# One attention and feed-forward layer in float32: constant rows filled by engines instead of DMAs, both first pairs stacked ahead, and three reorderings of the steady step

## The chip, the cores and the metric

The kernel runs on one core of a Trainium2 chip. The core has a matrix engine (TensorE, PE in the profile, with its weight loads as PEld), a vector engine (VectorE, DVE), an engine for activation functions (ScalarE, ACT), a general one (GpSimd, POOL), and a queue processor (SyncE, SP) that here only issues DMAs. Each engine works through its own instructions in the order in which the program gives them. They meet through semaphores.

The metric is the device time of one execution in microseconds. Three runs of the kernel before give a median of 858.41 us (858.38 to 859.41).

## The reference

The input is 32 sequences of 256 tokens with 128 features. What is computed, cut to what matters:

```python
def attn(x):                       # 16 heads of 8 features
    Q, K, V = heads(x @ Wq.T + bq), heads(x @ Wk.T + bk), heads(x @ Wv.T + bv)
    scores = Q @ K.T / sqrt(8)
    delta = t[:, None] - t[None, :]
    scores = where(delta < 0, -inf, scores) + where(delta < 0, 0, -delta)
    return heads_back(softmax(scores) @ V) @ Wo.T + bo

def ffn(x):                        # the weights are -8, 0 or 8, one scale for each output
    h = silu((x @ w1.T) * s1) * ((x @ w2.T) * s2)      # 128 -> 512
    h = gelu((h @ h1.T) * sh1)                         # 512 -> 512, exact gelu
    h = gelu((h @ h2.T) * sh2)                         # 512 -> 512
    return (h @ w3.T) * s3                             # 512 -> 128

x = layernorm(x + attn(x))
x = layernorm(x + ffn(x))
```

## The kernel before, in words

**Pairs and steps.** Two sequences make a pair: 512 tokens, four tiles of 128 (NT = 4). There are 16 pairs. `step(n)` (line 691) does the softmax of pair n, the row maxima of pair n+1, the projections of pair n+2, the last layer and last norm of pair n-2, and then the feed-forward layers of pair n-1. Every engine executes in program order, and that order is written out by hand: work is put into generators, and a `next()` puts its next piece of instructions where the call stands. `InOrder` (line 48) keeps the order of four engines as written, so that all their instructions carry line 56 in the profile.

**Scores.** Heads are worked in 8 groups of two. `qs[n % 2]` and `ks[n % 2]` (lines 109 and 110) are tiles of 128 partitions x 8 groups x 512 tokens, in which each half of the partitions holds one head's stacked rows: a high and a low part of q or k, which `project` and `halves` (315, 296) make and `stack` (306) moves in with 4 DMAs of 256 KB each per tensor; constant rows, which carry the distance term and a separation of the two sequences; and, in rows 62 and 63, the negated row maxima. With these rows one matmul yields finished scores. Before, the constant rows come about thus: DVE and POOL zero the four tiles (lines 111, 116, 670, 671), POOL makes small tiles of 4 x 512 (`constants`, 169), and 20 DMAs of 32 KB copy them into all groups (`stack_rows`, 204; `ones` for rows 62 and 63 of k).

**Row maxima.** `row_maxima(n, i)` (372), for i = 0 to 11, puts the scores of a third of two groups into a PSUM tile (`s`, from a pool of three) and has DVE reduce it into `m`. `maxima_to_rows(n)` (405) transposes `m` on PE (`pm`), splits it into a high and a low part on ACT and DVE (`mhi`, `mlo`) and moves them into q's rows 62 and 63 with four DMAs of 16 KB. Only then can pair n's softmax start.

**Softmax and outputs.** `weigh(n, i)` (424) makes the scores again, ACT takes the exponential (`e`), and POOL cuts the triangle. `outputs(n, a)` (462) is the product with the values (`pa`); for odd a, ACT copies it (`oT`), PE transposes it (`pt`) and DVE divides (`rec`, `on`). `finish(n)` (507) transposes (`pon`), copies (`onT`), multiplies by the output weights (`po`) and adds the input.

**Layer norms.** `layernorm` (265) has two pieces: statistics on DVE and a power on POOL, then the scaling on DVE. `first_norm` gives `x1`, `turn` transposes it, and `last(n)` (643) is the last layer (`pw` from `heven`), its scale (`yT`), a transposition back (`py`), the addition (`y`), the last norm (`z`, in four pieces in all) and the store.

**Feed-forward.** `feed(n)` (554) has twelve points at which other work is let in (`yield`): four in the first, gated layer, and four in each of the two inner layers. The weights are exact in the reduced float32r format; an activation is split into a high and a low part, so each product is two matmuls. An inner layer takes its outputs o in three passes, (0, 1), (2) and (3); the first pass does inner blocks k = 0, 1, 2 of output 0, then of output 1, and then k = 3 of both. The work let in is `rest()` (722) of `step`: the last outputs with their division, `maxima_to_rows(n + 1)`, `finish`, `project_values(n + 2)`, `first_norm`.

**Step 0** has no feed-forward work. It converts the weights to float32r and counts what differs (`inexact_weights`, 617; ACT casts and DVE `differ`, eleven pieces); the count (`pcount` on PE) decides the branch.

**The start** (lines 667 to 689): for pairs 0 and 1 in turn, project, zero, stack, add the constant rows, project the values; then the twelve row maxima of pair 0, `maxima_to_rows(0)`, the loads of the layers, and LEAD = 3 row maxima of pair 1.

Of the kernel before, what the change touches and what calls it, by code (L numbers as in the profile page):

```python
# [17 lines left out]
P = 128  # L18
# [11 lines left out]
W = 8  # L30
# [4 lines left out]
LEAD = 3  # L35
# [24 lines left out]
def tile_attn_ffn(  # L60
# [50 lines left out]
    vec.memset(qs[0].bitcast(F32), 0.0)  # L111
    ident = const.tile([P, P], F32, name="ident")
    make_identity(nc, ident)
    half = const.tile([P, NT], F32, name="half")
    nc.gpsimd.memset(half, -0.5)
    nc.gpsimd.memset(ks[0].bitcast(F32), 0.0)
# [14 lines left out]
    sctx = ctx.enter_context(ExitStack())  # L131
    setup = sctx.enter_context(tc.tile_pool(name="setup", bufs=1))
# [19 lines left out]
    act.dma_start(out=wv_sb, in_=wvT)  # L152
    act.dma_start(out=bv_sb, in_=bv.to_broadcast([P, D]))
    act.dma_start(out=bo_sb, in_=bo.to_broadcast([P, D]))
    for a in range(G):
        act.dma_start(
            out=wo_sb[C * HD * a : C * HD * (a + 1), :],
            in_=woT[:, :, a, :].rearrange("c d o -> (c d) o"),
        )
    for raw, dst in zip(raws, (wq_sb, wk_sb)):  # L160
        vec.tensor_copy(
            dst.rearrange("i (p d g) -> i p d g", p=2, g=W),
            raw.rearrange("i (g p d) -> i p d g", p=2, g=W),
        )
    vec.tensor_scalar(wq_sb, wq_sb, HD**-0.5, None, ALU.mult)
    vec.tensor_scalar(bq_sb, bq_sb, HD**-0.5, None, ALU.mult)


    def constants(step, one, value, lo, hi, nm):

        t = setup.tile([4, TOK], F32, name=nm)
        nc.gpsimd.iota(
            t, pattern=[[0, 2], [step, T]], base=0, channel_multiplier=0,
            allow_small_or_imprecise_dtypes=True,
        )
        nc.gpsimd.affine_select(
            out=t, in_=t, pattern=[[0, TOK]], base=1, channel_multiplier=-1,
            compare_op=ALU.is_ge, fill=0.0,
        )
        nc.gpsimd.affine_select(  # L180
            out=t, in_=t, pattern=[[0, TOK]], base=-one, channel_multiplier=1,
            compare_op=ALU.not_equal, fill=1.0,
        )
        u = setup.tile([4, TOK], F32, name=nm + "_mask")
        nc.gpsimd.memset(u, value)
        nc.gpsimd.affine_select(
            out=u, in_=u, pattern=[[0, 2], [1, T]], base=2 * P - lo, channel_multiplier=-P,
            compare_op=ALU.is_ge, fill=0.0,
        )
        nc.gpsimd.affine_select(  # L190
            out=u, in_=u, pattern=[[0, 2], [-1, T]], base=hi - 2 * P, channel_multiplier=P,
            compare_op=ALU.is_ge, fill=0.0,
        )
        nc.gpsimd.tensor_tensor(t, t, u, ALU.add)
        return t

    ones = setup.tile([2, TOK], F32, name="ones")
    nc.gpsimd.memset(ones, 1.0)
    const_rows = {
        "q": constants(-1, 0, 1.0, 0, 63, "qconst"),  # L200
        "k": constants(1, 1, BIG, 64, 127, "kconst"),
    }

    def stack_rows(dst, r, rows, eng):

        for p in range(2):
            eng.dma_start(
                out=dst.bitcast(F32)[64 * p + r : 64 * p + r + 2, :, :],
                in_=rows.unsqueeze(1).to_broadcast([2, W, TOK]),
            )  # L210

    def stack_constants(dst, nm, eng):
        for e in range(2):
            stack_rows(dst, W * e, const_rows[nm][2 * e : 2 * e + 2, :], eng)
# [157 lines left out]
    def row_maxima(n, i):  # L372
# [29 lines left out]
        for p in range(2):  # L402
            mask(s[:, p].rearrange("i h b j -> i (h b) j"), p, 0, 4)
        vec.tensor_reduce(
            mv[:, :, 2 * a : 2 * a + 2, :, 0], s, AX.X, ALU.max, negate=True
        )

    def maxima_to_rows(n):

        q, m = pairs[n]["q"], pairs[n]["m"]  # L410
        pm = work(f"pm_{n}")
# [419 lines left out]
```

## Time and profile before

| what | value |
|---|---|
| median of three runs | 858.41 us |
| the profiled execution's own time | 859.17 us |
| its span | 857.4 us, 17396 instructions |
| mean granted TensorE clock | 0.956 |
| busy: PE, DVE, ACT, POOL | 799.5, 635.0, 519.5, 270.9 us |
| first matmul of row maxima, pair 0 | 31.81 us |
| first matmul of the softmax, pairs 0, 1, 2 | 55.14, 91.23, 142.27 us |
| one steady step | 48.9 us |
| granted clock from 36.9 to 85.8 and from 85.8 to 134.6 us | 0.67, 0.83 |

The profiled execution's own time is 1.8 us longer than its span; the difference lies around the span. A step is the same to a few hundredths of a microsecond from pair 2 to pair 13, so one of them stands for all: the text uses the one from 377 to 426 us. The start up to about 135 us and the last two pairs are read apart.

### The profile page before, as it was taken

The numbers are of one execution on the slowest core, as the hardware profiler recorded it, in microseconds if no ns is written. First come the engines' busy times: TensorE is split into PE (matmuls) and PEld (weight loads), VectorE is DVE, ScalarE is ACT, GpSimd is POOL, SyncE is SP. The second block draws the span as 40 slices with busy tenths as digits, with TensorE's granted clock in tenths as the row PEclk, the third lists the DMA queues.
The fourth block names the chain that finished last, engine by engine and source line by source line (L and its number), as shares of the span: only waits on it lengthen the run. The fifth ranks groups of instructions, "written<-read, shape, count | busy, mean of one in ns | idle before, by whom it ended". The sixth has DMA issues, their size and how long they took to land.

```text
span 857.4 us, 17396 instructions
## 1 busy us (share of the span) xinstructions
PE 799.5 (93%) x7042; PEld 561.5 (65%) x7042; DVE 635.0 (74%) x1231; ACT 519.5 (61%) x713; POOL 270.9 (32%) x354
## 2 busy tenths in 40 slices
PE   4588999999999999999999999999999999999895
PEld 2355667676766767676766767676676767666673
DVE  3677677878778686878778787878778687874664
ACT  1026367666576676657676666657666666658462
POOL 9123332414232241414233240524224141424200
PEclk9558699999999999999999999999999999999998
DMA  6543240220405041140404032040504013000001
GB/s 142 128 147 86 45 101 16 61 67 14 102 14 114 14 101 26 38 90 14 103 13 112 16 74 54 14 102 14 115 13 111 5 48 68 14 5 13 1 1 29
DMA packets 40627, 48.16 MB, mean 56 GB/s; under 512 B 4376, under 2 KB 22040, under 8 KB 40536
## 3 DMA queue, kind: packets, MB, share of 16 engines
q1 hardware_dynamic: 38240, 44.13, 21.8%
q10 hardware_dynamic: 2296, 2.82, 1.4%
q8 instruction: 57, 0.93, 0.5%
q14 instruction: 34, 0.28, 0.1%
HBM read 7.48 MB, written 4.19 MB: 14 GB/s over the span
## 4 chain that ended last, share of the span: by engine, by line
PE 63%; DVE 24%; ACT 5%; issue 3%; DMA 2%; POOL 2%; ACTq 0%; DVEq 0%; POOLq 0%
PE peven L56 13%; PE s L56 9%; PE podd L56 9%; DVE m L56 9%; PE pw L56 8%; PE pa L56 8%; DVE h L56 5%; DVE h0w L56 3%; PE s_0d L56 2%; DVE z L56 2%; PE s_3d L56 2%; PE po L56 2%; PE pq L56 2%; PE pv L56 2%; ACT sg L56 1%
## 5 line engine op out<-in xcount | busy, mean ns | idle before, releaser
L459 POOL TENSOR_SCALAR_AFFINE_SELECT e<-e 128x512 f32<-128x512 f32 x128 | 82.5, 644 | 275.2 <-ACT e L56 275.2
L56 DVE TENSOR_REDUCE m<-s 128x4 f32<-128x1024 f32 x128 | 155.5, 1218 | 16.3 <-PE s L56 16.1
L56 ACT ACTIVATE e<-s 128x1024 f32<-128x1024 f32 x128 | 130.9, 1022 | 55.8 <-PE s L56 26.9
L56 PE MATMUL podd<-h,h_near 128*128 128x512 f32 x512 | 142.8, 414 | 3.8 <-DVE h L56 3.4
L56 PE MATMUL peven<-hodd,h_near 128*128 128x512 f32 x512 | 122.1, 395 | 0.0
L56 PEld LDWEIGHTS podd<-h,h_near 128*128 128x128 f32 x512 | 91.7, 190 | 37.1 <-DVE h L56 20.8
L56 PEld LDWEIGHTS peven<-hodd,h_near 128*128 128x128 f32 x512 | 95.9, 188 | 23.4
L56 ACT ACTIVATE hodd<-podd,sh 128x512 fp32r<-128x512 f32 x64 | 44.1, 689 | 76.3 <-PE podd L56 76.3
L56 DVE TENSOR_TENSOR heven<-evenw,heven 128x512 fp32r<-128x512 f32 x64 | 44.3, 693 | 48.0 <-ACT evenw L56 47.5
L56 PE MATMUL pw<-x1T,w_near 128*128 128x512 f32 x256 | 75.5, 418 | 0.9 <-DVE h0w L56 0.9
L56 PEld LDWEIGHTS s<-qs,ks 64*128 64x128 f32 x512 | 39.9, 191 | 55.3 <-issue 28.4
L56 PE MATMUL s<-qs,ks 64*128 64x256 f32 x512 | 67.0, 339 | 6.5 <-DVE m L56 6.4
L56 PE MATMUL pa<-e,vaug 128*32 128x256 f32 x1024 | 71.5, 393 | 0.1
L56 DVE SCALAR_TENSOR_TENSOR h0w<-pw,s,sg 128x512 f32<-128x512 f32 x64 | 47.9, 748 | 30.1 <-ACT sg L56 30.1
L275 POOL TENSOR_TENSOR rsa<-rsa,half 128x4 f32<-128x4 f32 x16 | 16.5, 1033 | 169.6 <-DVE rsa L56 169.5
L56 ACT ACT_TABLE_LOAD x47 | 60.3, 1283 | 3.4 <-issue 2.6
L56 PE MATMUL s<-ks,qs 62*128 62x256 f32 x512 | 59.1, 309 | 2.7 <-DVE m L56 1.4
L56 ACT ACTIVATE sg<-pw,s 128x512 f32<-128x512 f32 x64 | 43.8, 685 | 28.1 <-PE pw L56 27.7
L56 ACT ACTIVATE heven<-peven,sh 128x512 fp32r<-128x512 f32 x48 | 33.4, 696 | 39.0 <-PE peven L56 39.0
L576 POOL TENSOR_TENSOR h<-h0w,h 128x512 fp32r<-128x512 f32 x31 | 40.0, 1290 | 52.6 <-DVE h L56 52.6
L56 PEld LDWEIGHTS pw<-x1T,w_near 128*128 128x128 f32 x256 | 43.4, 188 | 18.1 <-ACT nothing L56 5.8
L56 DVE TENSOR_TENSOR hodd<-oddw,hodd 128x512 fp32r<-128x512 f32 x64 | 44.0, 688 | 13.9 <-ACT oddw L56 13.7
(145 smaller groups left out, 1425.8 us busy)
## 6 DMA issues: line engine op xcount, KB each, us to landing
qs<-qhi SPq DMA_DIRECT2D x32, 256.0 KB
qs<-qlo SPq DMA_DIRECT2D x32, 256.0 KB
ks<-khi SPq DMA_DIRECT2D x28, 256.0 KB
ks<-klo SPq DMA_DIRECT2D x28, 256.0 KB
x<-in_x_dram SPq DMA_DIRECT2D x16, 256.0 KB
out_dram<-z SPq DMA_DIRECT2D x16, 256.0 KB
ks<-khi ACTq DMA_DIRECT2D x4, 256.0 KB
ks<-klo ACTq DMA_DIRECT2D x4, 256.0 KB
```

The lines of the kernel that those rows point to most:

```text
L56: return lambda *args, **kw: self.tc.keep_in_program_order(call(*args, **kw))
L275: nc.gpsimd.tensor_tensor(rs, rs, half, ALU.pow)
L459: nc.gpsimd.affine_select(out=on_diagonal, in_=on_diagonal, pattern=[[0, on_diagonal.shape[1]], [1, P]], base=0, channel_multiplier=-1, co ...
L576: (nc.gpsimd if o < (1 if final else 2) else vec).tensor_tensor(h[:, 1, o, :], whole, h[:, 0, o, :].bitcast(F32), ALU.subtract)
```

## The change

It has these parts.

1. **Constant rows.** No tile is zeroed and no constant row is moved by DMA. POOL makes a column `row` (0 to 63, twice) and a tile `number` (the token number, 128 x 512). DVE works out eleven small columns from `row` and, with three instructions of 128 x 512 each for q and k, a tile whose per-partition rows are the constants. `fill` writes this tile into all 8 groups in one instruction of 128 x 4096: ks[0] by ACT, qs[0] and qs[1] by DVE, ks[1] by POOL.
2. **Both pairs first.** Projections and stacks of pairs 0 and 1 come first, then `project_values(0)`; the four loads of the output weights go behind the stacks on ACT's queue. The rearranged copies of Wq and Wk and the scaling of bq move from DVE to ACT.
3. **Maxima in halves.** `m` is laid out so that groups 0 to 3 and 4 to 7 can be moved apart. Pair 0's first half is moved after six row maxima, with `project_values(1)` and the layer loads beside it. LEAD is 2, and pair 1's maxima are moved within step 0's loop. Pair 2's row maxima run three places later in step 1 (LAG), with the last three among the inner layers. Step 0's weight conversion begins one place earlier. Pair 2's k stack goes by ACT's queue.
4. **Inner passes row by row.** For every inner block k and each part, the matmuls of the outputs follow one another.
5. **Division behind the last gate.** One more `yield` puts the division of the last outputs behind the fourth gated output; `project_values` goes ahead of `finish`.
6. **Last norm among inner layers.** From step 2 on, the last norm of pair n-2 (statistics, power, scaling, store) goes from the softmax loop to the end of `rest()`.

The diff, cut to its core:

```diff
+LEAD, LAG = 2, 3
...
-    vec.memset(qs[0].bitcast(F32), 0.0)
+    row = setup.tile([P, 1], F32, name="row")
+    for p in range(2):
+        nc.gpsimd.iota(
+            row[64 * p : 64 * p + 64, :], pattern=[[0, 1]], base=0, channel_multiplier=1,
...
+    number = setup.tile([P, TOK], F32, name="number_of")
+    nc.gpsimd.iota(
+        number, pattern=[[0, 2], [1, T]], base=0, channel_multiplier=0,
...
+    for raw, dst, scale in zip(raws, (wq_sb, wk_sb), (HD**-0.5, 1.0)):
+        act.activation(
+            dst.rearrange("i (p d g) -> i p d g", p=2, g=W),
+            raw.rearrange("i (g p d) -> i p d g", p=2, g=W), AF.Copy, scale=scale,
+        )
...
+    def constants(nm, col):
+        t = setup.tile([P, TOK], F32, name=f"{nm}const")
+        vec.tensor_scalar(t, number, col["lo"], col["value"], ALU.is_ge, ALU.mult)
+        vec.scalar_tensor_tensor(t, number, col["hi"], t, ALU.is_le, ALU.mult)
+        vec.scalar_tensor_tensor(t, number, col["slope"], t, ALU.mult, ALU.add)
+        fills[nm] = t, col["base"]
+
+    def fill(dst, nm, eng, groups=slice(0, W)):
+        t, base = fills[nm]
+        to = dst[:, groups, :]
+        t = t.unsqueeze(1).to_broadcast([P, groups.stop - groups.start, TOK])
+        if eng is act:
+            act.activation(to, t, AF.Identity, bias=base)
+        else:
+            eng.tensor_scalar(to, t, base, None, ALU.add)
...
+    constants("k", k)
+    fill(ks[0], "k", act)
...
-                for ks in ((0, 1, 2), (3,)):
-                    for o in os:
-                        for k in ks:
-                            product(
-                                ph[o], w[:, k, o * P : (o + 1) * P],
-                                [h[:, i, k, :] for i in parts], k == 0, k == KC - 1,
+                for k in range(KC):
+                    for i in parts:
+                        for o in os:
+                            pe.matmul(
+                                ph[o], lhsT=w[:, k, o * P : (o + 1) * P], rhs=h[:, i, k, :],
+                                start=k == i == 0, stop=k == KC - 1 and i == parts[-1],
                             )
...
+    ahead = project(0)
+    next(ahead)
+    constants("q", q)
+    fill(qs[0], "q", vec)
+    run(ahead)
+    stack(0, "q", sp)
+    stack(0, "k", act)
+    fill(ks[1], "k", nc.gpsimd)
+    ahead = project(1)
+    next(ahead)
+    fill(qs[1], "q", vec)
+    run(ahead)
+    stack(1, "q", sp)
+    stack(1, "k", act)
+    project_values(0)
...
-    for i in range(3 * G):
+    for i in range(6):
         row_maxima(0, i)
-    maxima_to_rows(0)
+    project_values(1)
+    maxima_to_rows(0, (0,))
     loaded = load_layers(once)
+    for i in range(6, 3 * G):
+        row_maxima(0, i)
+    maxima_to_rows(0, (1,))
     load_scales()
...
-            j = i if n else i + LEAD
-            if n + 1 < NPAIR and j < 3 * G:
+            j = i + {0: LEAD, 1: -LAG}.get(n, 0)
+            if n + 1 < NPAIR and 0 <= j < 3 * G:
                 row_maxima(n + 1, j)
...
-            if i in (0, 2, 4, 6) if n else i:
+            if i in ((0, 2) if n > 1 else (0, 2, 4, 6)) if n else i < 11:
                 next(settling, None)
...
+            if n == 0 and i == 3 * G - LEAD:
+                maxima_to_rows(1)
+        if n < 2:
+            run(settling)
...
-            stack(n + 2, "k")
+            stack(n + 2, "k", sp if n else act)
...
         def rest():
-            yield from side
+            for _ in range(3):
+                next(side)
+                yield
+            if n == 1:
+                for i in range(3 * G - LAG, 3 * G):
+                    row_maxima(2, i)
+                    yield
+            if 0 < n < NPAIR - 1:
+                maxima_to_rows(n + 1)
+            run(side)
             yield
-            if n + 1 < NPAIR:
-                maxima_to_rows(n + 1)
+            if n + 2 < NPAIR:
+                project_values(n + 2)
                 yield
             last_steps = finish(n)
             next(last_steps)
             yield
-            if n + 2 < NPAIR:
-                project_values(n + 2)
-                yield
             yield from last_steps
...
+            if n > 1:
+                yield
+                yield from settling
```

## The prediction

> **What bounds the kernel now.** I read the page first (shares, granted clock), then the chain of waits, then each engine's timeline of the start, of one steady step (377 to 426 us) and of the end, and the busy time in windows of the clock.
>
> The page:
>
> ```profile
> PE 799.5 (93%) x7042; PEld 561.5 (65%) x7042; DVE 635.0 (74%) x1231; ACT 519.5 (61%) x713; POOL 270.9 (32%) x354
> ...
> PEclk9558699999999999999999999999999999999998
> ```
>
> PE is nearly always busy, and a weight load stands beside every matmul. The second line shows the granted clock in 40 slices of 21.4 us: half in slices 2 and 3, low in slice 5. So the kernel has a slow start and then a long PE-bound part. A steady step, by windows (PE, PEld, DVE, ACT, POOL busy):
>
> ```profile
> 378.90:427.80 48.90, 48.06 (x442) 33.94 (x441) 38.46 (x77) 32.22 (x44) 15.63 (x20) 1.00 0.25 56
> ```
>
> Only 0.84 us of 48.9 is shown as PE idle, so relieving DVE can bring no more than PE's own stalls. They are read in PE's timeline, with the waits in brackets:
>
> ```profile
> 405.24 0.50 PE L56 MATMUL s<-qs,ks 64*128 64x256 f32 x4 [0.51 <-DVE m L56]
> ...
> 417.07 3.79 PE L56 MATMUL podd<-h,h_near 128*128 128x512 f32 x13
> 421.10 0.97 PE L56 MATMUL podd<-h,h_near 128*128 128x512 f32 x3 [0.23 <-DVE h L56]
> ```
>
> The first is the softmax loop waiting for DVE. The second hides more than its 0.23: 32 `peven` matmuls take 7.46 us in the chain, 0.233 each, so 16 `podd` from 417.07 should end at 420.8, but the chain shows `pon` only at 422.06. Some 1.0 us (after its short pipeline tail) is lost there, for k = 3. Why it is late stands in DVE's timeline:
>
> ```profile
> 417.71 0.69 DVE L56 TENSOR_TENSOR h<-h0w,h 128x512 fp32r<-128x512 f32 x1
> 418.32 0.35 DVE L56 RECIPROCAL rec<-pt 128x32 f32<-128x32 f32 x1
> 418.71 0.49 DVE L56 TENSOR_TENSOR on<-pt,rec 128x128 f32<-128x128 f32 x2
> 419.11 0.74 DVE L56 SCALAR_TENSOR_TENSOR h0w<-pw,s,sg 128x512 f32<-128x512 f32 x1
> ```
>
> The division stands 0.8 us in front of the fourth gated block. At the start, the chain:
>
> ```profile
> 13.15 8.12 DMA ks<-klo
> 21.26 0.02 issue
> 21.28 7.00 DMA ks<-kconst
> ...
> 31.95 2.65 issue
> 34.60 0.82 DVE vaug L56 x4
> 35.42 13.58 DVE m L56 x12
> ```
>
> Pair 0's stacks land at 21.3, its constant rows at 28.3, and behind them wait pair 1's projection (ACT's queue holds the constant DMAs) and the maxima.
>
> **The start (parts 1 to 3).** Removed: two memsets of 3.47 on DVE, two of 3.5 on POOL, 16 small POOL instructions of 0.5 to 1.3, 20 DMAs. Added on DVE before q can be stacked: eleven columns of one element (0.08 by the read-out of `differ`, 0.49 by the scaling of `bq_sb`; 0.1 taken, as rows without a wait are near it: 1.1); three instructions of 128x512 for k (0.43 as the `h` cast, 0.75 twice as `qlo`: 1.9); `xT` 0.7; three for q, 1.9; the fill. A fill of 128x4096 is not in the trace: eight casts of 0.43 make 3.4, `m`'s reduction slope (1.22 less 0.69 for 512 more: 1.03 ns) makes 4.3; 3.4 taken, as the form is nearer to the cast. From DVE's first instruction at 1.73 this ends at 10.8; `qlo` follows. ACT's fill: 1.02 for 1024 and 0.69 for 512 give 3.0, eight of 0.61 give 4.9; 3.0 taken; it ends near 10 and `qhi` and `khi` follow. Before, q's stacking was issued at 10.20, so it comes 0.6 later and should land at 21.5 (20.5 to 23; 2 MB, moved at 221 to 261 GB/s before too, less the constant DMAs). POOL's fill of ks[1] is 3.5 (its memset) to 10.3 (eight of its 1.29), 3.8 by the slope of its triangle cuts (0.644 to 1.09); ACT's queue then waits at pair 1's k DMAs, with the output weights' loads behind, but neither is needed for 20 us. PE's first row maxima move from 31.81 to 21.5, and DVE reduces from 22.9 on instead of 35.4.
>
> Moving the first half in between costs a bubble: `pv` 2.08 at half clock, `pm` 1.05, `mlo` 0.68, `vaug` 0.82, partly beside each other: 2.9 (2 to 4). Twelve maxima of 1.13 then end at 39.4 instead of 49.0. From there `pm` (1.05) and two maxima (1.05 to 1.2 each) lead to the softmax at 42.7 instead of 55.14: **-12.4** (-15.5 to -8).
>
> Step 0 itself gets one reduction (1.14) and `mlo` (0.6) more on DVE, but the last `differ` comes one place earlier: PE waits 3.38 for it at 81.34, half of which goes. Behind it `pm` (0.87 in the chain) is gone, `pv` covers the division (0.85), `po` waits 0.8 for `onT`, and k's four DMA issues (2.5) on ACT delay `oT` by 0.7 to 1. Together **-1.1** (-3 to +2).
>
> The clock. By windows (PE busy, granted clock, DMA share, GB/s):
>
> ```profile
> 75.48:78.89 3.41, 2.48 (x44) 1.00 0.00 0
> 78.89:82.31 3.42, 0.97 (x22) 1.00 0.90 216
> ...
> 99.37:102.79 3.42, 3.42 (x32) 0.50 0.29 81
> ```
>
> A window with 2.48 busy kept the clock, one with 0.97 was followed by half clock until 102.8. Now the idle time near `pcount` should be spread: two stretches of 1 to 1.5 us, about half busy, midway between these rows. If the clock stays, some 3 us of the tail and 5 of step 1's first 11.5 are saved, if not, nothing: **-4** (0 to -8).
>
> The Trainium skill ("TensorE: Matmul & The Clock Gate", Part 1) says that one busy window of about 3.4 us releases the clock. The windows between 92.5 and 99.4 were fully busy at half clock, so the trace does not bear that out; by the rule a fall would cost, as an estimate, under 2 us, and the sum would be some 2 us lower.
>
> Step 1: the same gated gain as below, and three reductions among its inner layers with three more PSUM tiles: **-0.5** (-1.5 to +2). Pair 2's stacks have three more places in which to land.
>
> **The steady step (parts 4 to 6).** Without the division, the fourth block's high part is there at 419.45 and its low part at 420.15. PE, row by row, wants them at 419.88 and 420.35: no stall. Taking `mlo`, division, `pon` behind `pv`, and `onT` in turn, the third pass of `podd` ends at 426.83 instead of 428.02: -1.19. Row by row adds no weight load, since each matmul has one already.
>
> The last norm takes from DVE's busy stretch (396.6 to 408.2) 0.86 + 0.37 + 0.17 and 1.46, so the 0.51 at 405.24 goes. They land here, between the `heven` low parts:
>
> ```profile
> 384.21 0.69 DVE L56 TENSOR_TENSOR heven<-evenw,heven 128x512 fp32r<-128x512 f32 x1 [2.01 <-ACT evenw L56]
> 385.37 0.69 DVE L56 TENSOR_TENSOR heven<-evenw,heven 128x512 fp32r<-128x512 f32 x1 [0.47 <-ACT evenw L56]
> 386.52 0.69 DVE L56 TENSOR_TENSOR heven<-evenw,heven 128x512 fp32r<-128x512 f32 x1 [0.46 <-ACT evenw L56]
> ```
>
> Statistics go behind the first, to 386.0; the second follows; POOL's power (1.01) ends at 387.1; `z` (1.11, as `x` without POOL beside it) at 388.2; then the third to 388.85, the cast to 389.3, the fourth to 389.95 instead of 388.5. PE's `pw` from `heven`, queued in front of all later scores, ends 0.71 later (0.98 with `z` at 1.38), and 0.14 of a wait behind it goes. DVE's next reductions start 1.4 late and are caught up by 396. The store waits behind `z` on SP and holds the next load of x some 6 us; that x is used a step later. Sum: -1.19 - 0.51 - 0.14 + 0.71 = -1.13; with 1.1 for pairs 2 to 13, **-13.2** (-22 to -2). Step 14 has no projection: **-0.9** (-1.3 to 0).
>
> **The end.** In step 15 PE waits 3.08 at 801.41 for `on`, and the clock halves for 3.4 us. With `pon` behind the first pass, that pass ends near 803 instead of 807.1; `onT` then stalls `po` 0.8, and the 0.85 at 812.78 goes, as `turn` falls behind 16 matmuls: **-4.0** (-5.3 to -1).
>
> **Sum.** -12.4 - 1.1 - 4 - 0.5 - 13.2 - 0.9 - 4.0 = -36.1. The profiled execution took 859.17 (span 857.4 and 1.8 around it): 823.1. The median of the runs is 0.76 lower, so 822.
>
> A rule that speaks against the change: the Trainium skill ("GPSIMD Engine Reference", section 8) says that POOL shares its SBUF interfaces with VectorE. The row agrees for casts (0.43, and 0.66 at 415.37 beside POOL); by it the first DVE fill would take 5.2 and the sum rise by 1.8.
>
> **Rivals.**
>
> - *The last norm blocks the inner layers* (slower). Place: DVE's queue ahead of the `heven` low parts. Against: DVE idles 2.01, 0.47 and 0.46 there. For: DVE cannot pass over `z`, which waits for POOL. If the whole norm counts, by its usual to longest rows 3.4 to 5.2 (0.87, 0.37, 0.41, 1.38, `z` 2.18 at 783.96), say 4.3 instead of 0.71 in 14 steps: +50, 872. It ends slower from 36.1 / 14 + 0.71 = 3.3 us a step.
> - *The start stays bound*, as stacks, fills or ACT's queue are late: pair 1's DMAs compete with pair 0's, the fills run slow beside POOL. Only 4 of 12.4 come: 831.
> - *The steady gain is taken by the next wait* (for `onT`, for PSUM tiles): step 1 and the steady terms at nothing, +14.6: 837. For it: PE shows only 0.84 idle.
> - *The clock falls as before*: 826, inside the forecast's own range, 814 to 830.
> - *The change does less than it says*, several terms at their poor ends at once: 838 to 856.
>
> **Chances.** Forecast 0.52, start bound 0.14, steady gain gone 0.18, the last rival 0.08, slower 0.08. The range 811 to 842 takes in all but about 2 in 10. A change under 0.2% (1.7 us) can't be told from none: faster 0.90, same 0.02, slower 0.08.
>
> **What would show it.** First row maxima near 21.5 and the softmax near 42.7; no `kconst` in the chain; no DVE release at `podd` or in the softmax loop; a new wait of `pw` for `heven` of 0.4 to 1; a step of 47.7; the clock at full after step 0, or half until some 10 us into step 1. A step over 48.9, or a start later than 50, would prove me wrong.

## The result, and the profile after

| | before | after |
|---|---|---|
| median of 6 runs each | 858.61 us (857.56 to 860.17) | 849.47 us (848.23 to 853.6) |
| profiled execution, its span | 859.17, 857.4 us | 849.53, 847.2 us |
| mean granted clock | 0.956 | 0.978 |

The ratio is 0.9905, with a 95% interval of 0.9889 to 0.9921: the change makes the kernel faster, by 9.1 us in the median and by 10.2 us in the span of the profiled executions, where 36.1 were forecast. The median lies above the forecast range of 811 to 842. The page of the changed kernel:

```profile
PE 789.4 (93%) x7046; PEld 553.1 (65%) x7046; DVE 642.9 (76%) x1245; ACT 525.1 (62%) x718; POOL 276.1 (33%) x341
...
PEclk9859999999999999999999999999999999999998
...
PE 73%; DVE 10%; ACT 4%; POOL 3%; issue 1%; DMA 1%; SPq 0%; ACTq 0%; POOLq 0%; DVEq 0%
PE podd L58 13%; PE pa L58 11%; PE s L58 10%; PE peven L58 8%; PE pw L58 8%; DVE heven L58 4%; POOL rsf L273 2%; PE s_2d L58 2%; PE s_3d L58 2%; PE s_1d L58 2%; PE s_0d L58 2%; PE po L58 2%; DVE z L58 2%; PE pt L58 2%; PE pk L58 2%; PE pq L58 2%
```

The last line counts the chain of work that ended last. The same line of the kernel before:

```profile
PE peven L56 13%; PE s L56 9%; PE podd L56 9%; DVE m L56 9%; PE pw L56 8%; PE pa L56 8%; DVE h L56 5%; DVE h0w L56 3%; PE s_0d L56 2%; DVE z L56 2%; PE s_3d L56 2%; PE po L56 2%; PE pq L56 2%; PE pv L56 2%; ACT sg L56 1%
```

PE is busy for 10 us less, and only one early slice is at half clock. The chain has two newcomers, DVE `heven` and POOL `rsf`, beside DVE `z`, while DVE `m`, `h` and `h0w` have left the line: the last norm in its new place now stands on the path. The times of each step's first softmax matmul say where the rest went (us; "mended" is the version with two places put right, below):

| stretch | before | after | forecast | measured | mended |
|---|---|---|---|---|---|
| start to pair 0's softmax | 55.14 | 49.74 | -12.4 | -5.4 | 42.66: -12.5 |
| steps 0 and 1 | 87.13 | 87.06 | -5.6 | -0.1 | 87.18: 0.0 |
| steps 2 to 13 | 586.30 | 583.52 | -13.2 | -2.8 | 568.76: -17.5 |
| step 14 | 46.93 | 47.66 | -0.9 | +0.7 | 46.39: -0.5 |
| step 15 to the end | 81.9 | 79.2 | -4.0 | -2.7 | 80.0: -1.9 |
| span | 857.4 | 847.2 | -36.1 | -10.2 | 825.0: -32.4 |

Of the 25.9 us that are missing, the two mended places bring back 22.2.

**The start.** DVE's timeline (start, duration, what):

```profile
5.22 0.69 DVE L58 COPY xT<-pxT 128x512 f32<-128x512 f32 x1 [0.95 <-PE pxT L58]
5.83 10.65 DVE L58 TENSOR_SCALAR qconst<-number_of,col_q_lo,col_q_value 128x512 f32<-128x512 f32 x1
16.52 0.82 DVE L58 SCALAR_TENSOR_TENSOR qconst<-number_of,col_q_hi,qconst 128x512 f32<-128x512 f32 x1
...
20.58 0.74 DVE L58 SCALAR_TENSOR_TENSOR qlo<-pq,bq_sb,qhi 128x512 fp32r<-128x512 f32 x1
```

and POOL's:

```profile
5.58 10.62 POOL L192 TENSOR_SCALAR ks<-kconst,col_k_base 128x4096 fp32r<-128x4096 f32 x1
```

One DVE instruction of 512 columns lasts 10.65 us, with no wait shown. It starts 0.25 us behind POOL's fill of ks[1] and ends 0.28 us behind it. q's stack, issued behind `qlo`, is 10 us later than forecast, and the first row maxima come at 30.02 instead of 21.5.

**The steady step** is 48.74 us instead of 48.86. PE's timeline of the one from 380 to 429:

```profile
410.37 3.97 PE L58 MATMUL podd<-h,h_near 128*128 128x512 f32 x16
...
428.74 1.44 PE L58 MATMUL pw<-heven,w_near 128*128 128x512 f32 x5
430.79 0.84 PE L58 MATMUL pw<-heven,w_near 128*128 128x512 f32 x2 [0.61 <-DVE heven L58]
431.85 0.49 PE L58 MATMUL pw<-heven,w_near 128*128 128x512 f32 x1 [0.22 <-DVE heven L58]
```

The stall inside `podd` is gone: 16 matmuls in one piece. But `pw`, which took 2.05 us before, takes 3.53 (from its first matmul to the next group's). The row of before, without a wait:

```profile
387.38 2.11 PE L56 MATMUL pw<-heven,w_near 128*128 128x512 f32 x8
```

DVE's timeline shows why:

```profile
425.56 0.69 DVE L58 TENSOR_TENSOR heven<-evenw,heven 128x512 fp32r<-128x512 f32 x1 [2.01 <-ACT evenw L58]
426.17 0.86 DVE L58 BATCH_NORM_STATS2 stf<-y 128x6 f32<-128x128 f32 x4
...
427.43 0.68 DVE L58 TENSOR_TENSOR heven<-evenw,heven 128x512 fp32r<-128x512 f32 x1
429.01 1.12 DVE L58 TENSOR_SCALAR z<-y,mvf,rsf 128x128 f32<-128x128 f32 x4 [0.91 <-POOL rsf L273]
430.05 0.68 DVE L58 TENSOR_TENSOR heven<-evenw,heven 128x512 fp32r<-128x512 f32 x1
430.65 0.42 DVE L58 CAST heven<-evenw 128x512 fp32r<-128x512 f32 x1
431.10 0.69 DVE L58 TENSOR_TENSOR heven<-evenw,heven 128x512 fp32r<-128x512 f32 x1
```

DVE idles 0.91 us for POOL's power (1.38 us) with two low parts queued behind `z`. The last low part ends 6.23 us after the first begins; before it was 4.31 (433.09 to 437.40).

**Steps 0 and 1.** PE's waits:

```profile
77.16 0.17 PE L58 MATMUL pcount<-found,ones_col 128*1 128x11 f32 x1 [1.04 <-DVE mlo L58]
...
80.92 0.66 PE L58 MATMUL pt<-ident,oT 128*128 128x128 f32 x4 [1.82 <-ACT oT L58]
...
84.05 1.16 PE L58 MATMUL po<-wo_sb,onT 128*128 128x128 f32 x8 [0.78 <-DVE onT L58]
...
89.71 0.79 PE L58 MATMUL s<-ks,qs 62*128 62x256 f32 x4 [1.73 <-ACT e_0d L58]
```

Before, one long wait stood here:

```profile
81.34 0.17 PE L56 MATMUL pcount<-found,ones_col 128*1 128x11 f32 x1 [3.38 <-DVE differ L56]
```

It has become many shorter ones. The windows of step 0 and step 1 (busy time of PE, PEld, DVE, ACT and POOL, granted clock, DMA share, GB/s), two rows of before and two of after:

```profile
55.14:91.23 36.09, 31.58 (x322) 21.55 (x319) 25.83 (x50) 20.38 (x28) 12.01 (x16) 0.74 0.56 147
91.23:142.27 51.04, 50.45 (x430) 35.31 (x430) 37.29 (x73) 29.73 (x40) 15.82 (x20) 0.89 0.23 54
...
49.74:85.79 36.05, 30.64 (x334) 19.87 (x331) 27.18 (x52) 20.52 (x28) 12.12 (x16) 0.82 0.30 73
85.79:136.80 51.01, 47.15 (x430) 32.85 (x430) 37.53 (x69) 29.49 (x40) 15.60 (x20) 0.97 0.24 54
```

In both steps together PE is busy for 77.8 us instead of 82.0, and idle for 9.3 instead of 5.1. Both kernels run at half clock at the beginning of step 0. The stretch of half clock that comes later fell from 20.5 us (82.3 to 102.8) to 3.4 (89.7 to 93.1). So PE's busy time fell by 4.2 us, and its waits rose by as much.

### The profile page after: what moved, and what is told of

Its sections match the earlier page's. It is cut to its first block, busy times and chain, and to the rows that moved or that the text cites. A ratio compares the mean times of both kernels' runs of the same rounds, so it can differ in the third digit from the quotient of the medians.

```text
span 847.2 us, 17426 instructions
## 1 busy us (share of the span) xinstructions
PE 789.4 (93%) x7046; PEld 553.1 (65%) x7046; DVE 642.9 (76%) x1245; ACT 525.1 (62%) x718; POOL 276.1 (33%) x341
## 4 chain that ended last, share of the span: by engine, by line
PE 73%; DVE 10%; ACT 4%; POOL 3%; issue 1%; DMA 1%; SPq 0%; ACTq 0%; POOLq 0%; DVEq 0%
PE podd L58 13%; PE pa L58 11%; PE s L58 10%; PE peven L58 8%; PE pw L58 8%; DVE heven L58 4%; POOL rsf L273 2%; PE s_2d L58 2%; PE s_3d L58 2%; PE s_1d L58 2%; PE s_0d L58 2%; PE po L58 2%; DVE z L58 2%; PE pt L58 2%; PE pk L58 2%; PE pq L58 2%
## 5 line engine op out<-in xcount | busy, mean ns | idle before, releaser
L462 POOL TENSOR_SCALAR_AFFINE_SELECT e<-e 128x512 f32<-128x512 f32 x128 | 84.7, 662 | 184.3 <-ACT e L58 156.2
L58 PE MATMUL podd<-h,h_near 128*128 128x512 f32 x512 | 131.4, 403 | 0.9 <-DVE m L58 0.5
L58 PE MATMUL s<-qs,ks 64*128 64x256 f32 x512 | 65.3, 334 | 1.1 <-DMA qs<-qhi 0.6
L58 PE MATMUL s<-ks,qs 62*128 62x256 f32 x512 | 55.1, 294 | 4.0 <-ACT e_0d L58 1.7
L273 POOL TENSOR_TENSOR rsf<-rsf,half 128x4 f32<-128x4 f32 x16 | 21.0, 1314 | 97.1 <-DVE rsf L58 97.1
```

Of the source, the lines that this page charges most:

```text
L58: return lambda *args, **kw: self.tc.keep_in_program_order(call(*args, **kw))
L273: nc.gpsimd.tensor_tensor(rs, rs, half, ALU.pow)
L462: nc.gpsimd.affine_select(out=on_diagonal, in_=on_diagonal, pattern=[[0, on_diagonal.shape[1]], [1, P]], base=0, channel_multiplier=-1, co ...
```

## Experiments: what holds DVE at the start

The theory is that POOL's fill and DVE's instruction exclude each other. The first edit takes the fill to ACT:

```diff
-    fill(ks[1], "k", nc.gpsimd)
+    fill(ks[1], "k", act)
```

> The fill of ks[1] goes from POOL to ACT; everything else as in the changed kernel (849.5 us). Theory A (POOL's 10.62 us fill holds DVE's first qconst instruction, 10.65 us, and with it q's stack): qconst's first instruction takes about 0.6 as kconst's did, q's stack is issued near 11 instead of 20.7, first row maxima at 20 to 23 us instead of 30.0, pair 0's softmax at 40 to 43 instead of 49.7, and the time 838 to 842. Rival (the start is held by its 2 MB of stacks and the DMA queues in any case): first row maxima not before 27, time 846 to 849. Second rival (the start comes early and is given back in step 0, whose end waits for pair 1 and for the weight count): first row maxima near 21, but step 1's softmax at 83 or later instead of 85.8, time 845 to 849.

Measured: 841.89 us, ratio 0.9812 (0.9796 to 0.9827). DVE's timeline:

```profile
5.83 0.54 DVE L58 TENSOR_SCALAR qconst<-number_of,col_q_lo,col_q_value 128x512 f32<-128x512 f32 x1
6.41 0.75 DVE L58 SCALAR_TENSOR_TENSOR qconst<-number_of,col_q_hi,qconst 128x512 f32<-128x512 f32 x1
```

The first row maxima come at 22.09 and pair 0's softmax at 42.81, 6.9 us earlier than in the changed kernel. The time falls by 7.6. The theory holds and both rivals fall: the first row maxima come 0.6 us from where they were forecast (21.5), and the gain reaches the end. The next question is what kind of exclusion it is. In this edit POOL does the fill in eight pieces:

```diff
+    for g in range(W):
+        fill(ks[1], "k", nc.gpsimd, slice(g, g + 1))
```

> The fill of ks[1] stays on POOL, in eight instructions of one group (128x512) instead of one of 128x4096. Theory A, first form (DVE's instruction is held until the POOL instruction that is running ends): pieces of about 1.3 us, qconst's first instruction at most 1.9, each further DVE instruction of that kind held by up to 1.3; first row maxima at 22 to 26, time 840 to 845. Theory A, second form (DVE is held as long as POOL has any work of this kind): qconst again near 10 us, first row maxima near 30, time 848 to 851. Rival (the wait is for data and not for POOL): the same as the second form, but with qconst ending at another moment than the last POOL piece.

Measured: 842.29 us, ratio 0.9819 (0.9803 to 0.9836). The first four rows are DVE's timeline, the last is POOL's:

```profile
5.85 0.70 DVE L58 TENSOR_SCALAR qconst<-number_of,col_q_lo,col_q_value 128x512 f32<-128x512 f32 x1
6.58 0.75 DVE L58 SCALAR_TENSOR_TENSOR qconst<-number_of,col_q_hi,qconst 128x512 f32<-128x512 f32 x1
7.37 1.06 DVE L58 SCALAR_TENSOR_TENSOR qconst<-number_of,col_q_slope,qconst 128x512 f32<-128x512 f32 x1
8.46 2.44 DVE L58 TENSOR_SCALAR qs<-qconst,col_q_base 128x4096 fp32r<-128x4096 f32 x1
...
5.58 13.40 POOL L192 TENSOR_SCALAR ks<-kconst,col_k_base 128x512 fp32r<-128x512 f32 x6
```

DVE is free, and its own long fill of qs (2.44) now holds POOL: six pieces take 13.40 us, four of them about 1.6 each and the two that meet the fills of qs 3.6 each. The time agrees with the first form of the theory, but the first piece ran from 5.58 to 7.15 and held DVE's instruction by 0.16 at most: less than "to the end of the running instruction" says. Three more edits, one run each, bear on this. The first has two pieces instead of eight:

```diff
+    for g in (0, 4):
+        fill(ks[1], "k", nc.gpsimd, slice(g, g + 4))
```

> The changed kernel with POOL's fill of ks[1] in two instructions of 128x2048. If DVE is held to the end of the POOL instruction that is running, when that is long: qconst's first instruction ends with the first piece, near 11 (5.2 us instead of 10.65), first row maxima at 24.5 to 27. If it is the fill as a whole: near 16.5 as before, first row maxima at 30. If a hold needs the whole 128x4096: 0.6 us, first row maxima at 22.

Measured: 848.33 us. Two rows of DVE's timeline and POOL's:

```profile
5.80 5.51 DVE L58 TENSOR_SCALAR qconst<-number_of,col_q_lo,col_q_value 128x512 f32<-128x512 f32 x1
11.34 4.07 DVE L58 SCALAR_TENSOR_TENSOR qconst<-number_of,col_q_hi,qconst 128x512 f32<-128x512 f32 x1
...
5.58 11.02 POOL L192 TENSOR_SCALAR ks<-kconst,col_k_base 128x2048 fp32r<-128x2048 f32 x2
```

Each long piece (5.45 and 5.58 us) holds one DVE instruction. The second hold, which the expectation had not counted, makes the first row maxima later than it said: 28.09 instead of 24.5 to 27. The next edit keeps the one long POOL instruction and gives DVE's first instruction another form, with two tensor inputs instead of one:

```diff
-        vec.tensor_scalar(t, number, col["lo"], col["value"], ALU.is_ge, ALU.mult)
+        vec.scalar_tensor_tensor(
+            t, number, col["lo"], col["value"].to_broadcast([P, TOK]), ALU.is_ge, ALU.mult
+        )
```

> The changed kernel with POOL's fill of ks[1] in one instruction, but qconst's first DVE instruction is written as SCALAR_TENSOR_TENSOR (two tensor inputs, the second one a column repeated) instead of TENSOR_SCALAR. If POOL's fill holds only DVE's one-input form: the three qconst instructions take 0.75 to 1.1 each and end near 8.4, and the next one-input instruction, the fill of qs[0], is the one that lasts until POOL ends near 16.2, or takes 2.4 and holds POOL instead; first row maxima at 22 (POOL held) or 27 to 29 (DVE held). If it holds any DVE instruction: the first qconst instruction takes 10 us or more as before, first row maxima at 30.

Measured: 852.51 us. DVE's timeline:

```profile
5.93 9.36 DVE L58 SCALAR_TENSOR_TENSOR qconst<-number_of,col_q_lo,col_q_value 128x512 f32<-128x512 f32 x1
```

The other form is held as well, though for 9.36 us and not for 10 or more: it ends at 15.29, 1.17 us ahead of POOL's end (16.46), and the first row maxima come at 28.76 instead of 30. The last edit has eight short pieces whose source is a repeated one, as in the long form (256 columns twice):

```diff
+    for g in range(W):
+        nc.gpsimd.tensor_scalar(
+            ks[1][:, g, :].rearrange("p (b j) -> p b j", b=2),
+            t[:, 0:T].unsqueeze(1).to_broadcast([P, 2, T]), base, None, ALU.add,
+        )
```

> The changed kernel with POOL's fill of ks[1] in eight instructions of 128x512, each with a repeated source (256 columns twice) as the long ones have it. If it is the repeated source that makes POOL hold DVE: the first qconst instruction ends with the first POOL piece near 7.2 (1.3 to 1.5 us instead of 0.6 to 0.7), the next ones are held likewise, qs's fill starts near 10 to 17. If it is the length of POOL's instruction: as with the plain pieces, 0.7, 0.75 and 1.06 us, qs's fill starts near 8.5, first row maxima near 22.

Measured: 841.63 us, with the first row maxima at 22.07. DVE's three instructions take 0.74, 0.75 and 1.06, as with plain pieces. So the repeated source is not what makes POOL hold DVE; among these fills the long ones hold it and the short ones hardly do. Length alone is not enough either. In the kernel before, POOL and DVE each zeroed a tile of 128x4096, and the two memsets overlapped for 2.8 us:

```profile
0.98 3.51 POOL L116 MEMSET ks<- 128x4096 f32 x1
...
1.73 3.47 DVE L56 MEMSET qs<- 128x4096 f32 x1 [1.73 <-PEq L816]
```

Neither was held: the later memsets of the same size, POOL's at 20.94 and DVE's at 31.21, ran apart and took the same 3.50 and 3.47 us. A memset only writes; whether it is the reading of the fills that makes the difference was not tried. Why pieces of 512 columns hold so little where 2048 hold for 5.5 us stays open; POOL's rows are rough in the profile.

## Experiments: the last norm's place

This edit undoes part 6 alone and puts the last norm back in the softmax loop:

```diff
-            if i in ((0, 2) if n > 1 else (0, 2, 4, 6)) if n else i < 11:
+            if i in (0, 2, 4, 6) if n else i < 11:
...
-        if n < 2:
-            run(settling)
+        run(settling)
...
-            if n > 1:
-                yield
-                yield from settling
```

> Part 6 alone is undone: the last norm is back in the softmax loop. Theory B (the last norm's power and scaling in front of DVE's heven low parts give back what row order and division gain): pw from heven in 2.05 us again instead of 3.53, the 0.51 wait in the softmax loop is back, a steady step of 47.9 to 48.2 instead of 48.68, time 839 to 843. Rival (row order and division bring nothing to the step, whatever podd shows): a step of 48.7 to 48.9, time 849 to 853.

Measured: 840.19 us, ratio 0.9797 (0.9780 to 0.9813), with a step of 48.09. PE's timeline:

```profile
379.04 2.11 PE L58 MATMUL pw<-heven,w_near 128*128 128x512 f32 x8
396.89 0.50 PE L58 MATMUL s<-qs,ks 64*128 64x256 f32 x4 [0.50 <-DVE m L58]
```

It is as theory B says: `pw` is whole again, and the wait of 0.5 is back in the loop. Parts 4 and 5 together (row order, the division's place and `project_values` ahead of `finish`) do bring 0.77 a step (48.86 to 48.09), and part 6 as written costs 0.65 of it. The next edit keeps part 6 and takes out one `yield`, so that the statistics stand ahead of the first low part:

```diff
             if n > 1:
-                yield
                 yield from settling
```

> The last norm stays among the inner layers, but its statistics run one slot earlier, with the first norm's scaling, in DVE's idle 2 us ahead of the first heven low part; its scaling comes one slot earlier too. Theory B: POOL's power is over before DVE needs it, pw from heven is at most 0.7 longer than before (2.05), a step of 47.5 to 48.0, time 833 to 841. Rival (the sum of DVE's work there is too long in any place): the first low part is late instead, pw waits as long (3.3 to 3.6), a step of 48.5 to 48.9, time 847 to 852.

Measured: 833.95 us, ratio 0.9720 (0.9704 to 0.9735), with a step of 47.39. DVE's timeline:

```profile
417.78 0.86 DVE L58 BATCH_NORM_STATS2 stf<-y 128x6 f32<-128x128 f32 x4
...
419.88 0.69 DVE L58 TENSOR_TENSOR heven<-evenw,heven 128x512 fp32r<-128x512 f32 x1 [0.75 <-ACT evenw L58]
420.49 1.11 DVE L58 TENSOR_SCALAR z<-y,mvf,rsf 128x128 f32<-128x128 f32 x4
421.51 1.37 DVE L58 TENSOR_TENSOR heven<-evenw,heven 128x512 fp32r<-128x512 f32 x2
423.03 0.43 DVE L58 CAST heven<-evenw 128x512 fp32r<-128x512 f32 x1
423.49 0.69 DVE L58 TENSOR_TENSOR heven<-evenw,heven 128x512 fp32r<-128x512 f32 x1
```

The statistics now fill 1.3 of the 2.0 us in which DVE waited for ACT, the power runs beside a wait and the first low part, and `z` waits for nothing. The last low part ends 4.30 us after the first begins, as before the change. One slot is worth 1.35 us a step (48.74 to 47.39). The next version has both mended places together:

> The changed kernel with both mended places: the fill of ks[1] on ACT, and the last norm's statistics one slot earlier. If the two losses are independent (one lies in the start, one in each steady step), their gains add: 849.5 - 7.6 - 15.5 = 826.4, 825 to 828. Rival (the shorter start only moves pair 0 and 1 into a wait that the other edit lengthens, or the clock falls): 829 to 834.

Measured: 827.02 us (826.27 to 827.16), ratio 0.9627 (0.9606 to 0.9648). The two gains, 7.6 and 15.5 us, add up to within 0.7.

## Experiments: row order and division

On top of that version, this edit brings back the old order of the inner passes:

```diff
-                for k in range(KC):
-                    for i in parts:
-                        for o in os:
+                for ks in ((0, 1, 2), (3,)):
+                    for o in os:
+                        for k in ks:
```

> As the version with both mended places, but the inner passes in the order of before (blocks 0, 1, 2 of output 0, then of output 1, then block 3 of both). If the division's place is what frees podd: a step of 47.4 to 47.6 (47.39 with row by row). Rival (row by row is what frees it): the stall of before comes back, podd waits 0.5 or more for h, a step of 47.9 to 48.4.

Measured (one run): a step of 47.52 instead of 47.40, so row by row is worth 0.12. The next edit puts the division ahead of the gate again:

```diff
             pe.transpose(po[:, t].rearrange("i c k -> i (c k)"), oT[:, t * P : (t + 1) * P], ident)
-        yield
         rec = mp.tile([P, NT, C, 2], F32, name=f"rec_{n}_{r}", tag="rec")
...
-                next(side)
+                next(side, None)
```

> As the version with both mended places, but the division of the last outputs stands ahead of the fourth gated block again, with row by row kept. If the division's place is what frees podd: the low part of the fourth block is 0.8 us late, podd waits 0.5 to 0.8, a step of 47.9 to 48.3. Rival (row by row, which wants the fourth block's low part 0.23 later, is enough by itself): a step of 47.4 to 47.6.

Measured (one run): a step of 48.07. PE's timeline:

```profile
399.87 3.04 PE L58 MATMUL podd<-h,h_near 128*128 128x512 f32 x12
403.12 1.47 PE L58 MATMUL podd<-h,h_near 128*128 128x512 f32 x4 [0.22 <-DVE h L58]
```

The division's place is worth 0.67, and the stall shows again as a small wait and four slow matmuls. With 0.70 for the last norm out of the loop (48.09 to 47.39), 0.12 + 0.67 + 0.70 = 1.49 accounts for the 1.46 between 48.86 and 47.40.

## Experiments: steps 0 and 1

It was open why 5.6 us of forecast gave nothing, with both places mended too. A run from above says what the half clock costs here. The single run with DVE's first instruction in the other form has the same code in steps 0 and 1 as the changed kernel, and PE's waits in the two steps are the same within 0.3 us each, but its later stretch of half clock lasts from 87.8 to 101.4, 13.6 us instead of 3.4. Its step 1 takes 54.99 us (PE busy for 51.52) instead of 51.01 (47.15). So 10 us more of half clock, all inside step 1, cost 4.0 us. In the version with both places mended, which also has that code, half clock holds for 10.2 us, from 73.4 to 80.2 and from 83.6 to 87.0, around the border of the two steps. In both steps PE is busy for 2.0 us longer and waits 2.0 less, and they take 87.18, as in the changed kernel (87.06), though a part of this may come from step 0's beginning, where half clock holds for 10.1 us instead of 12.7. So what the clock is worth depends on where the stretch lies: 4 us inside step 1, and little shows at the border, where PE waits for others.

The first edit is aimed at one of these waits. ACT's copy `oT` stands behind four DMA issues of pair 2's k stack:

```profile
80.28 0.58 ACT L58 COPY oT<-pa 128x512 f32<-128x512 f32 x1 [3.04 <-DMA ks<-khi]
```

The edit puts the copy ahead (two pieces of the last outputs before the stack):

```diff
+        if n == 0:
+            next(side)
+            next(side)
         if n + 2 < NPAIR:
             stack(n + 2, "q")
...
-                next(side)
+                next(side, None)
```

> As the version with both mended places, and in step 0 ACT's copy oT stands ahead of pair 2's four k stack DMAs on its queue. Theory C (step 0's end gives back what its clock gained, because oT waits 3.04 us behind those DMAs): pt no longer waits 1.82, step 1's softmax comes 1.5 to 2.5 us earlier, time 1.5 to 2.5 below the version without this edit. Rival (the next wait takes its place: on ACT's exponentials and the norm of pair 0 at the beginning of step 1): step 1's softmax earlier by 1.5 to 2, step 2's by under 0.5, time within 0.5.

Measured: 828.04 us, ratio 0.9648 (0.9626 to 0.9669), 1.0 us more than the version without this edit. The theory forecast 1.5 to 2.5 less and the rival no change within 0.5, so both missed. Step 1's softmax does come earlier, at 76.79 instead of 78.65, but step 2's comes at 130.84 instead of 129.84. PE's timeline names the wait that took over, and it isn't the one that the rival named:

```profile
83.29 0.80 PE L58 MATMUL s<-ks,qs 62*128 62x256 f32 x4 [4.13 <-DMA qs<-qlo]
```

Pair 2's first row maxima now wait for the landing of its stack. So the next edit puts its maxima two places later still:

```diff
-LEAD, LAG = 2, 3
+LEAD, LAG = 2, 5
```

> The version with both mended places, oT ahead of the k stack, and pair 2's row maxima five places later in step 1 instead of three. Theory C2 (with oT first, the next thing late is pair 2's stack, which lands near 83.3 and on which PE then waits 4.13): two more places give it 4 us, the wait goes, step 2's softmax at 126 to 128.5 instead of 129.84, time 823 to 826. Rival (five row maxima among the inner layers of step 1 cost as much there, in DVE's queue and PSUM tiles): step 2's softmax at 129 to 131.5, time 826.5 to 829.

Measured: 832.38 us, ratio 0.9705 (0.9690 to 0.9719), slower than both forecasts. Step 2's softmax comes at 129.70, where the rival had it, and the wait for the stack is gone, but step 2 itself takes 51.68 us instead of 47.40. Of these 4.28 us, 2.94 are one wait of PE at 137.04: its `s_0d` waits for DVE's reduction `m`, which DVE reaches late. A stretch of half clock from 138.2 to 141.7 follows it. The opposite edit leaves out the lag (`LEAD, LAG = 2, 0`, without `oT` ahead):

> The version with both mended places, but pair 2's row maxima start with step 1 again instead of three places later. Pair 2's stack is issued from 68 on and lands near 81 to 83 while step 1 starts at 78.65, so PE should wait 3 to 5 us for it at its first row maxima; step 1's end has no maxima among its inner layers, which gives 0.5 to 1 back. Step 2's softmax at 131.5 to 134 instead of 129.84, time 829 to 831. Rival (the three maxima among the inner layers cost more than the wait): step 2's softmax at 128 to 129.5, time 825 to 826.5.

Measured (one run): 827.95 us. PE's timeline:

```profile
81.46 0.61 PE L58 MATMUL s<-ks,qs 62*128 62x256 f32 x4 [3.12 <-DMA qs<-qlo]
```

The wait is there, and step 1 takes 52.75 us instead of 51.19. It began 0.81 earlier, so step 2's softmax, at 130.59, is only 0.75 later than with LAG = 3, between the two forecasts. So the lag saves 1.56 us of step 1 where the wait that it removes is 3.12. Is step 0 bound by DVE, to which the change gave one more reduction? The next edit compares only 32 of every 512 columns:

```diff
-                    differ, whole, 1.0, part.bitcast(F32), ALU.mult, ALU.not_equal,
+                    differ[:, 0:32], whole[:, 0:32], 1.0, part.bitcast(F32)[:, 0:32],
+                    ALU.mult, ALU.not_equal,
```

> The version with both mended places, but the count of inexact weights compares only the first 32 of each 512 columns, so DVE's eleven differ instructions in step 0 fall from 0.67 to about 0.1 us each (the rest of the comparison is left out). If step 0 is bound by DVE: 11 x 0.57 = 6.3 us less, step 1's softmax 4 to 6.5 us earlier (at 72 to 74.7 instead of 78.65) and the time 821 to 824. Rival (it is bound by ACT or by the chain of reductions, scores and PSUM tiles): step 1's softmax at 76.5 to 78.6, time 825 to 827.

Measured (one run): 827.39 us. The eleven `differ` instructions fall from 0.68 to 0.19 us each, 5.4 us less work for DVE, yet PE reaches `pcount` at 69.49 (68.97 with the whole count), step 1's softmax at 77.74 (78.65) and step 2's at 129.33 (129.84). With DVE as the bound, step 1's softmax would have come at 72 to 74.7. So DVE's work is not what sets step 0; what is left, ACT's exponentials and casts with PE's scores, was not taken apart. The last question is the start's move in halves. One edit moves the maxima in one piece and has the loads of the layers between the sixth and the seventh maxima:

```diff
     for i in range(6):
         row_maxima(0, i)
-    project_values(1)
-    maxima_to_rows(0, (0,))
     loaded = load_layers(once)
     for i in range(6, 3 * G):
         row_maxima(0, i)
-    maxima_to_rows(0, (1,))
+    maxima_to_rows(0)
     load_scales()
+    project_values(1)
```

> The version with both mended places, but pair 0's maxima are moved in one piece after all twelve (the layers' loads stay after the sixth, pair 1's values are projected behind the move). If moving in halves costs its bubble and gains nothing, since the second half has the same chain behind it: the 3.3 us between the sixth and the seventh reduction go, pair 0's softmax at 39.5 to 41.5 instead of 42.66, time 824 to 826 if step 0 keeps its 36.0. Rival (what stood in the bubble, pv and the additions, is paid behind the move instead, and the row DMAs land later behind the layers' loads): softmax at 42.5 to 44, time 826.5 to 829.

Measured (one run): 834.01 us. It answers another question. SP issued the loads from 3.8 to 6.6 us, ahead of the stacks that precede them in the program; why is not shown. The first k stack's issue on ACT's queue then took 10.04 us for two DMAs, the first row maxima came at 29.84 and the softmax at 49.40. The next edit has the loads behind the move:

```diff
-    maxima_to_rows(0, (1,))
+    maxima_to_rows(0)
+    loaded = load_layers(once)
     load_scales()
+    project_values(1)
```

> The version with both mended places (827.0 us), but pair 0's maxima are moved in one piece after all twelve, the layers' loads behind that move as before, and pair 1's values projected behind it. If moving in halves costs its bubble and gains nothing: pair 0's softmax at 39 to 41 instead of 42.66 and step 0 at 36 to 37 us, time 824 to 826. Rival (the halves pay because the loads and pv lie in the bubble): softmax at 40 to 42, but step 0 is longer by what was moved into it, since the loads land while the softmax runs, 37.5 to 40; time 827 to 830.

Measured: 825.86 us (824.6 to 826.34), ratio 0.9614 (0.9593 to 0.9636). The softmax is at 41.59 instead of 42.66 and steps 0 and 1 take 87.24, unchanged: the halves cost 1.1 us at the start and give nothing back. It is the fastest version, though its interval overlaps that of the version with halves.

## Why the prediction was wrong, point by point

- **The start, -12.4, measured -5.4.** The step that failed is the one on POOL's fill of ks[1]: "3.5 to 10.3 ... but neither is needed for 20 us". Its duration, 10.62, was just above these bounds. Its price was sought in who needs the result, not in what it does to DVE beside it. The text took a slowdown from `h` casts beside POOL (0.43 to 0.66) and named 1.8 us for it, in a sentence apart and outside the sum; DVE lost 10. The rest of the term stands: in the mended version, with the fill elsewhere, the first row maxima come at 21.94 (21.5 forecast) and the softmax at 42.66 (42.7), although the move in halves, a part of that term, cost 1.1 us.
- **Step 0's end -1.1, the clock -4, step 1 -0.5: together -0.1.** The clock was freed as forecast, and PE is busy for 4.2 us less. Two things in the sum failed. The terms of the steps themselves left out waits of 4.87 us: 0.73 for `m` at `pm`, 0.58 for a DMA into qs and 2.27 for ACT's exponentials at the beginning of step 1, 0.51 for `m` and 0.78 for `onT` among its inner layers. And the clock's gain was added to them as if PE alone set the pace. The runs with the same code show that 10 us more of half clock inside step 1 cost 4.0 us, while 10.2 us of it at the border left the two steps as long as 3.4 us did. Which engine sets the pace of step 0 stays open: with DVE's work cut by 5.4 us it came out at 34.99 us instead of 35.99, and it differs by up to 0.9 between runs with the same step 0.
- **Steady step, -1.13, measured -0.12.** Division and row order were put at 1.19 and gave 0.77 to 0.81: the mechanism was right, the size a third too large. The 0.51 and 0.14 came as forecast (0.70 together). The mis-sized term that took the gain is the last norm among the `heven` parts: +0.71 was forecast and +1.35 to +1.48 measured. The fourth low part was to end 1.45 later and ended 1.92 later, of which the power is 0.37 (1.38 instead of 1.01). Of this PE felt 1.48, since there was 0.44 of slack where 0.74 was assumed.
- **Step 14 and the end.** Step 14 has the same norm: +0.7 instead of -0.9. At the end, -2.7 instead of -4.0, the 3.08 and the 0.85 went as forecast, but PE waits 2.24 for `h0w` at 814.84 instead of 0.86, behind `z` and two low parts of `heven` in DVE's queue: the same norm in the last inner layer. The earlier slot did not help there (80.0 us): in the mended version PE waits 1.06 for `evenw` and 1.68 for `h0w`.
- **The rivals.** Two of them were true at once, "the start stays bound" and "the steady gain is taken by the next wait", the second by the mechanism of the slower rival at a third of its price (1.35 of 4.3). Each was priced with all else at its best (831, 837). The last rival, several terms at their poor ends at once (838 to 856), holds the measured 849.47. It had a chance of 0.08 and named no mechanism, and the range, which ended at 842, left most of it out.

## What to carry to other kernels

Before an idle engine is given a long instruction, look at what its neighbours run in that time, and give it short pieces or another engine where one of them is on the path. A small step put into an in-order queue is priced by the wait inside it: statistics, a trip to another engine, then scaling should be split so that the trip falls into a gap that is there anyway; one slot decided 1.35 us of 48. A faster clock is worth its time where PE sets the pace (4 us inside step 1) and little where PE waits for others (at the border of steps 0 and 1), so its gain is not to be added before the waits of that stretch are listed.

## What the runs showed of the hardware

A POOL fill (TENSOR_SCALAR) of 2048 or 4096 columns stops a DVE instruction that starts just after it for 5.5 and 10.65 us. Pieces of 512 columns (1.57 us each) hardly do: the DVE instructions beside them lost 0.31 us at most. A DVE fill of 4096 columns (2.44 us) stretches a POOL piece from 1.56 to 3.6 us. Two memsets of 128x4096, which only write, ran beside each other for 2.8 us and kept their 3.5 us. The Trainium skill ("SBUF — State Buffer", "Who interferes with whom") says that GpSimd has only a pair of ports that VectorE shares, and that where a VectorE instruction uses both pairs, whoever issues first has the shared one for the whole instruction while the other blocks. The long fills agree, in both directions. The short pieces don't: the same DVE instruction that the long fill held would, by the rule, have been held by the first piece to 7.15, and it was through at 6.55. The hold ended 0.28 us behind POOL for the form with one tensor input and 1.17 us ahead of it for the one with two. POOL's fill costs 2.6 us per 1024 columns (10.62 for 4096) where ACT's costs 0.9 (3.71) and DVE's 0.6 (2.35).
